# Two stacked attentions on one core: who empties PSUM around the turns between the layers

## Chip, cores and metric

The kernel runs on one core of one Trainium2 chip. The metric is device time in microseconds (us), launch to end; 3021.95 us is the median of three runs before the change (3021.81 to 3022.91). The profiled execution took 3022.45 us, with a span of 3020.7 us, and TensorE had 0.997 of its full clock.

## The reference, cut to what matters

The input `x` is float32, 8 images x 64 channels x 64 x 64, so N = 4096 positions per image.

```python
# layer 0
f, g, hh = Wf @ x + bf, Wg @ x + bg, Wh @ x + bh        # 8, 8 and 64 channels
beta = softmax(f.T @ g, axis=keys)                      # 4096 x 4096 per image
x = x + hh @ beta.T
# layer 1
xn = group_norm(x, 8 groups) * gamma + beta_
q, k, v = split(w_qkv @ xn + b_qkv)                     # 64 channels each
attn = softmax(q.T @ k * 64**-0.5)                      # 4096 x 4096 per image
out = x + w_proj @ (attn @ v) + b_proj
```

## The kernel before, in words

**Tiles.** An image lies in SBUF as 128 partitions x 2048 columns: the 64 channels of the first half of the positions, and below them those of the second half. The 2048 columns are four *chunks* of 512 queries (`CW`), for both halves at once. A chunk takes 16 *steps* `t` (`NT`). One step handles 128 keys of each half: TensorE makes four 128 x 512 blocks of scores, ScalarE turns them into exponentials in an SBUF tile `e` (128 x 2048; the pool holds six, `ppool`), TensorE multiplies them with the values and adds into an accumulator in PSUM (`weigh`), and VectorE adds `e` into a running sum `esum` for the softmax's denominator.

**PSUM.** Of the eight banks, 1 to 6 form three pairs that scores and projections use in turn (`pair`); banks 0 and 7 hold the accumulators (`outer`). Layer 1 needs both, one for each 64 keys; layer 0 needs one and swaps them from chunk to chunk, so that the other serves as a seventh bank for scores.

**Order.** The layers are interleaved: layer 0 of images 0 and 1, then layer 1 of image 0, layer 0 of image 2, layer 1 of image 1, and so on; layer 1 of image 7 ends it. So from 565 us on a *period* repeats: 64 steps of layer 0 of image b, then 64 steps of layer 1 of image b-1. Six times layer 1 is followed by layer 0, and seven times layer 0 by layer 1; these are the *turns*. In the trace the first such period lies from 565.2 to 936.4 us: layer 0 of image 2 until about 706.8 us, layer 1 of image 1 after it. (Layer 1 of image 0 comes ahead of it, from 336.3 us on.)

**Who sets the order.** TensorE's order is written out by hand: each matmul is tied behind the one before (`in_order`). In layer 1 a step issues its scores (L958), its exponentials (L961), and then, in `ended`, the work that is due and the `weigh` of the step before. Layer 0 works in groups of six or seven 512-column blocks of scores, then the due work, then `weigh`. Work beside the main loop is put on a list with a step number (`at_step`) and taken when its step comes (`take`), at most one piece that needs a pair of banks per step; layer 0 looks one step ahead (L976).

**What runs beside layer 1 of an image b-2**, by the step numbers in `before` of both layers: for layer 0 of image b, `begin` at step 25 (it projects f and g with 8 matmuls in `project_all`, L594, copies the result out of PSUM by ScalarE at L608, and splits it on VectorE into a rounded and a rest part, `high`, with two instructions), `spread` at step 28 (twelve transfers that lay f and g out), and `values` at steps 36, 38, 43 and 45; for layer 1 of image b-1, the group norm's statistics from step 20 on, and from step 35 in steps of 7 `project` (L747), followed two steps later by `values`. `values` (L335) is 16 small matmuls into a pair of banks, and one copy of 128 x 512 out of it. The copy goes to VectorE when no pair is lent (`lent is None`), which is always so in layer 1's steps; in layer 0's steps it goes to ScalarE.

**The end of a chunk.** `finish` (L361) calls `total`: in layer 1 two ScalarE copies take the accumulators out of PSUM (L790, L791), and VectorE adds them later, in `halves`. The remaining pieces (`halves`, `transposed`, `reciprocals`, `result`) are due over the next steps; `transposed` and `reciprocals` send small transfers, and `result` waits for `r`, the reciprocals spread by two transfers of 128 KB.

VectorE instructions are recorded by one helper (L141), TensorE's matmuls by another (L151); they are told apart by their tiles. The trace holds two records for each float32 matmul, so that the 8 matmuls of a layer 1 step's scores show as x16.

Of the kernel before, what the change touches and what calls it, by code (L numbers as in the profile page):

```python
# [68 lines left out]
def fast_path(  # L69
# [19 lines left out]
    nc = tc.nc  # L89
# [23 lines left out]
    lent = None  # L113

    def pair():
        nonlocal turn
        if lent is not None:
            return pairs[lent]
        turn += 1
        return pairs[turn % 3]  # L120
# [27 lines left out]
    vector = InOrder()  # L148
# [176 lines left out]
    class Attention:  # L325
# [12 lines left out]
        def values(self, src, w, c):  # L338

            ps = pair()  # L340
            for t in range(TPC):
                for m in range(2):
                    for h in range(2):
                        matmul(
                            ps[ts(m, C), h, ts(t, C)], src[ts(h, C), ds(t * P + m * C, C)],
                            w[ts(h, C), :], start=True, stop=True,
                        )

            first_ = self.kind == self.b == c == 0
            copy = vector.tensor_copy if lent is None or first_ else nc.scalar.copy  # L350
            copy(
                self.vt[:, :, ts(c, TPC), :],
                ps[:, :, 0 : TPC * C].rearrange("k p (t c) -> k p t c", c=C),
            )

        def finish(self, acc, esum, c, index):

            n = f"{self.name}_{c}"
            raw = work.tile([P, CW], F32, tag="raw", bufs=4, name=f"raw_{n}")
            other = self.total(raw, acc)  # L360
            zt = small.tile([P, QP], F32, tag="zt", bufs=4, name=f"zt_{n}")  # L361
            width = CW // 2
            r = four = None

            def halves():
                if other is not None:
                    vector.tensor_add(raw, raw, other)
                vector.tensor_add(esum[:, 0], esum[:, 0], esum[:, 1])

            def transposed():  # L370


                nonlocal four
                both_ = work.tile([P, 8 * QP], F32, tag="zs", name=f"part_{n}")
                part = both_[:, 0:32]
                four = both_[:, 32:].rearrange("p (a k) -> p a k", k=QP)
                vector.tensor_reduce(
                    part, esum[:, 0].rearrange("p h (i b) -> p b (h i)", b=32),
                    axis=AX.X, op=ALU.add, apply_transpose=True,
                )  # L380
                for a in range(4):
                    nc.sync.dma_start(four[:, a, :], part[ts(a, 32), :])

            def sums(spare):

                z = banks[:, spare, :]

                zs = work.tile([P, width], F32, tag="zs", name=f"zs_{n}")
                for h in range(2):
                    for i in range(2):  # L390
                        row = 32 * (2 * h + i)
                        matmul(
                            z[row : row + 32, 0:width], ones[:, 0:32], esum[:, 0, h, ts(i, width)],
                            start=True, stop=True, tile_position=(0, row),
                        )
                nc.scalar.copy(zs, z[:, 0:width])
                for h in range(2):
                    for i in range(2):
                        row = 32 * (2 * h + i)
                        nc.sync.dma_start(zt[row : row + 32, :], zs[row : row + 1, :])  # L400

            def broadcast():
                nonlocal r
                r = work.tile([P, CW], F32, tag="r", name=f"r_{n}")

            def reciprocals():
                rt = stash[:, ts(index, QP)]
                if four is not None:
                    vector.tensor_reduce(
                        zt, four.rearrange("p a k -> p k a"), axis=AX.X, op=ALU.add  # L410
                    )
                vector.reciprocal(rt, zt)
                broadcast()
                dealt = recips[index]
                nc.sync.dma_start(dealt, rt)
                for h in range(2):
                    row = dealt[ts(h, C), :].rearrange("p e -> (p e)")
                    nc.sync.dma_start(r[ts(h, C), :], row.partition_broadcast(C))

            def result():  # L420
                vector.tensor_mul(raw, raw, r)
                self.residual(raw, c)

            return halves, transposed, sums, reciprocals, result
# [52 lines left out]
    class Layer0(Attention):  # L477
# [4 lines left out]
        def before(self):  # L482

            def begin():
                if self.b == 1:
                    self.own(F32R)
                else:
                    self.parts = proj.tile([P, 2, NH], F32R, tag="fg", name=f"fg_{self.name}")  # L490
                    if self.b != 2:
                        self.own_vt()
                self.f, self.g = self.parts[:, 0, :], self.parts[:, 1, :]
                self.st = small.tile(
                    [P, NC, nc.vector.BN_STATS_DIM], F32, tag="st", name=f"st_{self.name}"
                )
                if self.b > 0:
                    self.project_all()
                else:
                    self.project_direct()  # L500
                    self.project(0, (1,))

            def rest():
                self.project(1)
                with tc.issue_after(self.sent.ins):
                    for b in (1, 2):
                        load_x(b)

            if self.b == 0:
                return [(-1, begin, True), (0, rest, True)] + [  # L510
                    (
                        (-1, 1, 5, 8)[c],
                        lambda c=c: self.values(x_tiles[0][:, ts(c, CW)], wh, c),
                        True,
                    )
                    for c in range(NC)
                ]


            s = 28 if self.b == 1 else 25  # L520
            return [(s, begin, True), (s + (4 if self.b == 1 else 3), self.spread, False)] + [
                (
                    (36, 38, 43, 45)[c],
                    lambda c=c: self.values(x_tiles[self.b][:, ts(c, CW)], wh, c),
                    True,
                )
                for c in range(NC)
            ]
# [114 lines left out]
        def weigh(self, acc, e, t, p, start, stop, cols):  # L643
            for h in range(2):
                matmul(
                    acc[0][ts(h, C), cols], self.vt[:, p, t, :], e[:, h, cols],
                    start=start, stop=stop,
                )

        def total(self, raw, acc):  # L650
            nc.scalar.copy(raw, acc[0])
            return None

# [5 lines left out]
    class Layer1(Attention):  # L659
# [124 lines left out]
                        e[ts(m, C), h, cols], start=start, stop=stop,  # L784
                    )

        def total(self, raw, acc):

            other = work.tile([P, CW], F32, tag="r", name=f"other_{self.name}")
            nc.scalar.copy(raw, acc[0])  # L790
            nc.scalar.copy(other, acc[1])  # L791
            return other
# [17 lines left out]
    seq = [(at, c) for at in order for c in range(NC)]  # L810
# [38 lines left out]
    acc = esum = first = None  # L849
# [96 lines left out]
    while i < len(seq):  # L946
        at, c = seq[i]
        tight = i < 2 * NC
        if at.kind == 1:
            for j in range(0, 2 * NT, 2):  # L950
                now = i * NT + j // 2
                due, taken = take(now)
                batch, left = ready, []
                t = j // 2
                new = []
                both_ps = [pair(), pair()]
                for p in range(2):
                    at.scores(both_ps[p], t, p, c)  # L958
                e = ppool.tile([P, 2, 2, CW], F32, tag="e", name=f"e_{at.name}_{c}_{t}")
                for p in range(2):  # L960
                    nc.scalar.activation(e[:, p], both_ps[p], AF.Exp, scale=at.scale)  # L961
                    new.append((i, j + p, e, slice(0, CW)))
                ended()
            i += 1
            continue
# [6 lines left out]
        u = 0  # L972
        while u < len(units):
            k, t = units[u][:2]
            now = k * NT + t
            due, taken = take(now + 1)  # L976
            wide = 7 if closed == 0 and taken != BANK else 6
            batch, left = due_part(ready, wide - (2 if taken == PAIR else 0))
# [8 lines left out]
            if taken == PAIR:  # L987
                lent = 0 if room[-1] == 7 else 2
# [6 lines left out]
            while group:  # L995
                (k, t, p, h), bank = group[0]
                first_ = 2 * p + h
                n_ = min(4 - first_, len(group))
                at, c = seq[k]
# [11 lines left out]
            lent = None  # L1011
        i = last
    now = len(seq) * NT
# [390 lines left out]
```

## Time and profile before

| engine | busy, us | share of the span |
|---|---|---|
| TensorE, matmul | 2984.6 | 99% |
| TensorE, weight load | 1076.8 | 36% |
| VectorE | 2601.0 | 86% |
| ScalarE | 2055.7 | 68% |
| GpSimd | 15.7 | 1% |

| instruction | count | mean, ns |
|---|---|---|
| VectorE `esum` + `e`, 128 x 2048 | 629 | 2288 |
| ScalarE exponential in layer 1, 128 x 1024 | 1024 | 1023 |
| VectorE copy PSUM to `v`, 128 x 512 | 28 | 694 |
| VectorE copy PSUM to `vt`, 128 x 512 | 25 | 695 |
| ScalarE copy PSUM to `v`, 128 x 512 | 8 | 589 |
| ScalarE copies of the accumulators in layer 1 | 31 + 31 | 588, 598 |
| VectorE split of f and g, two instructions | 8 and 7 | 688 and 1285 |

Read it thus: a busy TensorE row is nearly full here whatever happens, because a matmul that has been issued early counts as busy; so a stall shows better in the weight loads (PEld), in the list of waits, and in the distance between one step's exponentials and the next's. VectorE and ScalarE rows are real busy times.

### The profile page before, as it was taken

Reading aid. Unit: us, or ns where it says so; the run is one execution under the profiler, and the core shown is the slowest. Engines: PE = TensorE matmul, PEld = TensorE weight load, DVE = VectorE, ACT = ScalarE, POOL = GpSimd, SP = SyncE. Lnnn points to the kernel's source line nnn. Section 1 sums busy time; section 2 is a strip of 40 time slices with the busy share of each in tenths; the row PEclk is TensorE's granted clock in tenths of the full one; section 3 lists DMA queues with packets and bytes.
Section 4 is the critical chain, followed back from the end, with each engine's and each line's share of the span. In section 5 each row is a group of like instructions: output and inputs, shape, how many; then the busy total and the mean of one; then the engine's idle time right before and its main releaser. Section 6 shows DMA issues by size and latency. Waiting matters only on the chain.

```text
span 3020.7 us, 58290 instructions
## 1 busy us (share of the span) xinstructions
PE 2984.6 (99%) x25629; PEld 1076.8 (36%) x25629; DVE 2601.0 (86%) x1705; ACT 2055.7 (68%) x1979; POOL 15.7 (1%) x40
## 2 busy tenths in 40 slices
PE   8999999999999999999999999999999999999998
PEld 3333333333333333333333333333333333333333
DVE  7999977899878998789987899879997799976776
ACT  6877655786557866578655885568855588566554
POOL 2000000000000000000000000000000000000000
PEclk9999999999999999999999999999999999999999
DMA  2100020100201002010020100200002000010000
GB/s 65 43 8 15 12 51 19 29 1 9 54 19 29 1 13 51 20 29 1 16 51 19 26 1 16 51 23 22 1 16 54 19 8 1 17 23 15 9 15 13
DMA packets 77141, 66.93 MB, mean 22 GB/s; under 512 B 54048, under 2 KB 54080, under 8 KB 75088
## 3 DMA queue, kind: packets, MB, share of 16 engines
q1 hardware_dynamic: 75792, 63.01, 8.7%
q8 instruction: 202, 3.31, 0.5%
q14 instruction: 59, 0.48, 0.1%
q0 software_dynamic: 768, 0.09, 0.0%
q10 hardware_dynamic: 320, 0.04, 0.0%
HBM read 39.84 MB, written 12.32 MB: 17 GB/s over the span
## 4 chain that ended last, share of the span: by engine, by line
PE 89%; DVE 6%; ACT 2%; issue 2%; DMA 0%; SPq 0%; DVEq 0%; ACTq 0%
PE banks L151 89%; DVE esum_l L141 5%; DVE vt_l L141 1%; ACT e_l L961 1%; ACT e_l L1002 1%; DMA x<-in_x_dram 0%; ACT other_l L791 0%; DMA moments<-mv_l 0%; DVE raw_l L141 0%; DVE x L141 0%; DVE st_l L141 0%; ACT full_l L573 0%; DMA zt_l<-zs_l 0%; DVE high_l L141 0%; DMA group_l<-moments 0%
## 5 line engine op out<-in xcount | busy, mean ns | idle before, releaser
L141 DVE TENSOR_TENSOR esum_l<-esum_l,e_l 128x2048 f32<-128x2048 f32 x629 | 1439.4, 2288 | 255.1 <-ACT e_l L961 230.2
L961 ACT ACTIVATE e_l<-banks 128x1024 f32<-128x1024 f32 x1024 | 993.8, 1023 | 733.7 <-PE banks L151 733.7
L151 PE MATMUL banks<-e_l,v_l 64*64 64x512 f32 (+1 forms) x8780 | 1094.0, 587 | 0.0
L1002 ACT ACTIVATE e_l<-banks 128x2048 f32<-128x2048 f32 (+3 forms) x727 | 954.5, 1375 | 180.1 <-PE banks L151 166.4
L151 PE MATMUL banks<-kq_l 64*64 64x512 f32 (+1 forms) x8448 | 1005.3, 586 | 5.7 <-ACT e_l L1002 4.7
L151 PE MATMUL banks<-e_l,vt_l 128*64 128x512 f32 (+1 forms) x4056 | 830.5, 550 | 0.0
L141 DVE TENSOR_TENSOR kq_l<-kq_l,e_l 128x2048 f32<-128x2048 f32 x252 | 577.3, 2291 | 24.8 <-DVE kq_l L141 0.9
L151 PEld LDWEIGHTS banks<-e_l,v_l 64*64 64x64 f32 (+1 forms) x8780 | 347.3, 134 | 593.7 <-issue 517.9
L151 PEld LDWEIGHTS banks<-kq_l 64*64 64x64 f32 (+1 forms) x8448 | 325.3, 134 | 600.3 <-issue 556.7
L151 PEld LDWEIGHTS banks<-e_l,vt_l 128*64 128x64 f32 x4056 | 267.3, 136 | 468.7 <-issue 449.2
L151 PE MATMUL banks<-fg_l 32*128 32x512 f32 x1792 | 206.8, 459 | 6.5 <-ACT e_l L1002 3.3
L141 DVE TENSOR_TENSOR esum_l<-e_l,e_l 128x2048 f32<-128x2048 f32 x45 | 102.3, 2274 | 85.7 <-ACT e_l L961 85.7
L151 PEld LDWEIGHTS banks<-fg_l 32*128 32x128 f32 x1792 | 85.6, 182 | 188.3 <-ACT e_l L1002 138.0
L141 DVE TRANSPOSE_TENSOR_REDUCE part_l<-esum_l 128x32 f32<-128x1024 f32 x38 | 74.5, 1961 | 0.0
L141 DVE TENSOR_TENSOR esum_l<-esum_l 128x1024 f32<-128x1024 f32 x44 | 53.7, 1221 | 0.4
L141 DVE TENSOR_TENSOR raw_l<-raw_l,r_l 128x512 f32<-128x512 f32 x63 | 43.2, 686 | 0.0
L141 DVE TENSOR_TENSOR kq_l<-e_l,e_l 128x2048 f32<-128x2048 f32 x18 | 41.2, 2287 | 1.4 <-ACT e_l L1002 1.4
L141 DVE TRANSPOSE_TENSOR_REDUCE part_l<-kq_l 128x32 f32<-128x1024 f32 x18 | 35.2, 1957 | 0.2
L141 DVE TENSOR_TENSOR vt_l<-vt_l,e_l 128x2048 f32<-128x2048 f32 x14 | 32.1, 2291 | 1.2
L764 ACT ACTIVATE kq_l<-banks,kqb 64x256 f32<-64x256 f32 x64 | 30.0, 469 | 1.2
L151 PEld LDWEIGHTS banks<-wkq_wvp,kq_l 64*64 64x64 f32 x1024 | 19.4, 134 | 28.0 <-DVE vt_l L141 18.0
L151 PE MATMUL banks<-wkq_wvp,kq_l 64*64 64x64 f32 x1024 | 21.4, 221 | 7.5 <-DVE vt_l L141 7.5
(126 smaller groups left out, 475.6 us busy)
## 6 DMA issues: line engine op xcount, KB each, us to landing
r_l<-recips SPq DMA_DIRECT2D x126, 128.0 KB
kq_l<-kq_l SPq DMA_DIRECT2D x64, 128.0 KB
out_dram<-raw_l SPq DMA_DIRECT2D x62, 128.0 KB
x<-in_x_dram SPq DMA_DIRECT2D x30, 256.0 KB
fg_l<-fg_sent_l SPq DMA_DIRECT2D x24, 256.0 KB
fg_l<-fg_sent_l SPq DMA_DIRECT2D x48, 128.0 KB
part_l<-part_l SPq DMA_DIRECT2D x228, 4.0 KB
fg_sent_l<-high_l SPq DMA_DIRECT2D x28, 128.0 KB
```

Source lines behind the costliest of these rows:

```text
L141: it = getattr(nc.vector, name)(*args, **kwargs)
L151: in_order(nc.tensor.matmul(*args, **kwargs))
L764: nc.scalar.activation(self.q[ts(h, C), cols[1]], ps[other, 1, 0:width], AF.Identity, bias=k1["kqb"][other, :],)
L961: nc.scalar.activation(e[:, p], both_ps[p], AF.Exp, scale=at.scale)
L1002: nc.scalar.activation(e.rearrange("k p h n -> k (p h) n")[:, first_ : first_ + n_, :], banks[:, bank : bank + n_, :], AF.Exp, scale=at.scale,
```

## The change

It does four things.

1. `values` leave PSUM by ScalarE in layer 1's steps as well; only the very first copy of the program stays on VectorE. That moves 28 copies to `v` and 24 to `vt`, so that TensorE's next use of the pair does not stand behind VectorE's queue.
2. `begin` for images 2 to 7 moves from step 25 of layer 1 to its step 0, and is taken at the turn; `spread` keeps step 28 in the list.
3. At the turn from layer 0 to layer 1 the last `weigh` of layer 0, and what is due, are issued before the first scores of layer 1, so that f and g are projected where layer 0's last work is.
4. At the turn from layer 1 to layer 0 VectorE takes both accumulators: one copy and one addition that reads the second accumulator from PSUM, in place of two ScalarE copies and a later addition.

```diff
-            first_ = self.kind == self.b == c == 0
-            copy = vector.tensor_copy if lent is None or first_ else nc.scalar.copy
+            copy = vector.tensor_copy if self.kind == self.b == c == 0 else nc.scalar.copy
...
-            other = self.total(raw, acc)
+            other = self.total(raw, acc, index)
...
-            s = 28 if self.b == 1 else 25
-            return [(s, begin, True), (s + (4 if self.b == 1 else 3), self.spread, False)] + [
+            s, spread = (28, 32) if self.b == 1 else (0, 28)
+            return [(s, begin, True), (spread, self.spread, False)] + [
...
-        def total(self, raw, acc):
-
+        def total(self, raw, acc, index):
+            if seq[index + 1][0].kind == 0:
+                vector.tensor_copy(raw, acc[0])
+                vector.tensor_add(raw, acc[1], raw)
+                return None
             other = work.tile([P, CW], F32, tag="r", name=f"other_{self.name}")
             nc.scalar.copy(raw, acc[0])
             nc.scalar.copy(other, acc[1])
...
                 new = []
+                if batch and seq[batch[0][0]][0].kind == 0:
+                    for r in batch:
+                        weigh(*r, now)
+                    for u in due:
+                        u[2]()
+                    due, batch = [], []
                 both_ps = [pair(), pair()]
```

More of the change, by code (lines that the diff above doesn't have):

```diff
@@ L785, in weigh, with total @@
                     )
-        def total(self, raw, acc):
+        def total(self, raw, acc, index):
+            if seq[index + 1][0].kind == 0:
+                vector.tensor_copy(raw, acc[0])
+                vector.tensor_add(raw, acc[1], raw)
+                return None
             other = work.tile([P, CW], F32, tag="r", name=f"other_{self.name}")
```

## The prediction

> **What bounds the kernel now.** I read the page's shares first, then the list of waits, then the timeline of one period.
>
> ```profile
> PE 2984.6 (99%) x25629; PEld 1076.8 (36%) x25629; DVE 2601.0 (86%) x1705; ACT 2055.7 (68%) x1979; POOL 15.7 (1%) x40
> ...
> PE 89%; DVE 6%; ACT 2%; issue 2%; DMA 0%; SPq 0%; DVEq 0%; ACTq 0%
> ```
>
> TensorE sets the pace: 89% of the chain of waits. VectorE's 6% is what a change to VectorE's queue can speak to, not its 86% of busy time. The waits from 430 us on (past the start) say who holds TensorE:
>
> ```profile
> ACT e_l L961 <- PE banks L151: 695.3, 461, 3.2
> ...
> PEld banks L151 <- DVE vt_l L141: 18.0, 12, 1.8
> ...
> PEld banks L151 <- DVE v_l L141: 8.5, 19, 0.7
> DVE raw_l L141 <- ACT other_l L791: 8.0, 6, 1.3
> ...
> PE banks L151 <- DVE vt_l L141: 7.5, 12, 1.0
> ```
>
> Columns: total us, times, longest. ScalarE waits 695 us for TensorE in layer 1, so it has room there. TensorE waits for one thing that is avoidable: VectorE's copies out of PSUM. The twelve `vt` waits are two in each of six layer 1 stages. The timeline shows the larger one (first VectorE, then ScalarE, then weight loads; start, duration, in brackets the idle time before):
>
> ```profile
> 832.51 2.29 DVE L141 TENSOR_TENSOR esum_l<-esum_l,e_l 128x2048 f32<-128x2048 f32 x1
> 834.72 2.00 DVE L141 TRANSPOSE_TENSOR_REDUCE part_l<-esum_l 128x32 f32<-128x1024 f32 x1
> 836.58 2.31 DVE L141 TENSOR_TENSOR esum_l<-esum_l,e_l 128x2048 f32<-128x2048 f32 x1
> 838.75 0.74 DVE L141 COPY vt_l<-banks 128x512 f32<-128x512 f32 x1
> ```
> ```profile
> 837.79 1.94 ACT L961 ACTIVATE e_l<-banks 128x1024 f32<-128x1024 f32 x2 [1.96 <-PE banks L151]
> 842.89 1.94 ACT L961 ACTIVATE e_l<-banks 128x1024 f32<-128x1024 f32 x2 [3.15 <-PE banks L151]
> 846.85 1.02 ACT L961 ACTIVATE e_l<-banks 128x1024 f32<-128x1024 f32 x1 [2.02 <-PE banks L151]
> ```
> ```profile
> 839.54 0.56 PEld L151 LDWEIGHTS banks<-wkq_wvp,kq_l 64*64 64x64 f32 x32 [1.84 <-DVE vt_l L141]
> ```
>
> The copy of 0.74 us sits behind an end-of-chunk reduction and a 2.3 us addition; the next `values` needs the pair. ScalarE meanwhile waits 3.15 us for scores.
>
> **What the Trainium skill says.** "PSUM — Partial Sum Buffer", section Engine vs sequencer instructions: "ScalarE/VectorE/GpSimdE queues are strict FIFO." The lines above agree: the copy starts when the addition ahead of it ends. "Perfetto Trace Analysis", section Optimizing Scalar/DVE Operations, gives ScalarE the smaller access overhead on PSUM (51 against 125 ns). The trace agrees in direction: 589 against 694 ns for the same 128 x 512 copy; I use these. "TensorEngine Tiling (Array Packing)", section Key Properties, says that a change of tiling mode drains TensorE; at the turns below a switch costs some 0.1 to 0.2 us.
>
> **Part 1, values by ScalarE.** In layer 1 the exponentials start 3.43 us apart (e.g. 853.71 to 857.15). A step with `project` or with an undelayed `values` takes 3.86 to 3.90; I take 3.88. The distances around the eight `values` of a period are 3.90, 5.10, 3.96, 3.90, 4.36, 3.90, 3.84 and 3.90, with small after-effects (3.48 for 3.43, twice). Excess: 1.22 + 0.08 + 0.48 + 2 x 0.05, about 1.9 us. Six stages have it (layer 1 of images 0 to 5): **11.4 us**. Bounds: 7.5 us, the matmul row's waits for `vt`; and 17.8, the weight loads' 26.5 us of waits for `vt` and `v` less the 0.28 that each of the 31 has between any two groups. The ScalarE copy itself I cost at nothing: it goes in behind the step's 1.94 us of exponentials, ahead of the next step's scores; ScalarE idles 1.49 us in a plain step, and about 1.9 when `values` lengthens it. 0.59 fits. Behind the copy wait the next exponentials, which wait for scores anyway. The pair comes free about 3.7 us after the step's scores start (1.16 to the first exponential, 1.94, 0.59), while the next `values` cannot come before 3.88 + 1.72 = 5.6.
>
> **Part 4, the turn from layer 1 to layer 0.** The matmuls there:
>
> ```profile
> 568.53 2.80 PE L151 MATMUL banks<-e_l,vt_l 128*64 128x512 f32 x12
> 571.26 1.19 PE L151 MATMUL banks<-fg_l 32*128 32x512 f32 x7
> 572.38 2.80 PE L151 MATMUL banks<-e_l,vt_l 128*64 128x512 f32 x12
> 575.11 0.93 PE L151 MATMUL banks<-fg_l 32*128 32x512 f32 x7
> ```
>
> A group's seven blocks of scores take 0.66 before the next `weigh` when banks are free (586.38 to 587.05). The third group takes 1.12 (571.26 to 572.38): its later blocks wait for exponentials that ScalarE began at 568.83, after its two accumulator copies (567.89 to 568.97). Without these they start near 568.0 and end before 571.26: 0.45 us. The fourth group's 0.86 stays, since ScalarE (seven blocks in 3.22 us plus 0.59 of waiting for scores) is the slower one while groups are short. The second group's 1.39 stays too; it waits for the first exponentials. So **0.43 x 6 = 2.6 us**, between 0 and the whole lost here, 0.7 + 0.45 + 0.2 = 1.4, times six, 8. VectorE gets 0.69 + 0.69 (the same two kinds at the kernel's end take 0.69 each) for an addition of 0.69. In the built instruction order they come behind `halves`, which ends at 567.67; so bank 0 is free near 568.4, as now (568.49), and the 0.69 more fits into the 1.34 us for which VectorE waited there.
>
> **Parts 2 and 3, the turn from layer 0 to layer 1.** At step 25 the projection lengthens a step from 3.43 to 4.61 (exponentials at 794.52 and 799.13): 1.18 us removed. At the turn it costs from 0.86 (a step's eight scores matmuls run four at a time, 0.86 for each four; the projection's eight lie in eight tiles, so once) up to 1.3. No wait hides it: TensorE is full from 703.18 to 714.44. But the order scores, `weigh`, scores, `weigh`, scores, `weigh` becomes scores, projection, the whole `weigh`, two sets of scores; layer 1's first scores lose their 0.16 (1.88 for 1.72) and layer 0's last `weigh` its 0.15 (2.30 for ten half blocks at 0.215). My sum: 10.40 us (0.44 + 0.2 + 0.86 + 0.2 + 5.16 + 0.1 + 3.44, the 0.1s and 0.2s estimates for switches from these rows) for 9.55 + 1.18 = 10.73. **0.33 x 6 = 2.0**, and 0.3 at the seventh turn, which has no projection; bounds -1 and 4. The first scores now have no `weigh` to hide their exponentials, but `weigh` of the first step comes only after two sets of scores, 3.44 us on, and the exponentials end 1.16 + 1.94 = 3.10 us after the first set starts.
>
> VectorE: `high` and its split (1.97 us) move from step 25 to the turn, where VectorE is about 10 us behind (the last layer 0 exponential ends at 705.64, its addition at 716.26). The first layer 1 addition then ends near 723.6 for 721.6. With six `e` buffers, the exponential of layer 1's seventh step needs the first one back, at 729.3: 5 us of room. The spread's transfers are now issued some 80 us earlier, about 725 to 736, near `r` of layer 0's first chunk. Twelve of them drained at about 200 GB/s from 806 to 817 before; I find `r` landing near 740, and VectorE not at its product before 744. Cost nothing.
>
> **Sum**: 11.4 + 2.6 + 2.0 + 0.3 = 16.3, so **3005.7 us**. TensorE's matmuls are the same in number and shape.
>
> **Rivals.**
> - *The wait moves to ScalarE.* If its copies delay exponentials, or the pair is held by the queue ahead of them, part 1 gives little. For: the copy is in order behind 1.94 us of work. Against: 733.7 us of ScalarE's waiting for TensorE. Time: only the 4.9 us of the other parts, less 0 to 4 of new waits: 3017 to 3021.
> - *VectorE blocks at the turn.* If `r` comes 10 us late behind the spread, VectorE stands, the six `e` buffers fill, and ScalarE and TensorE stop for some 5 us each period: 3005.7 + 6 x 5 = 3036. For: VectorE is full from 716 to 771. Against: the 4 us of room worked out above, and 5 us in the buffers.
> - *More than counted*: part 1 at its upper 17.8 and part 4 at 6: 3021.95 - 26 = 2996.
>
> **Chances.** Forecast 0.78, wait moved 0.09, slower 0.06, more than counted 0.07. Range 3000 to 3013: parts 1 and 4 at their likely spread. Faster by over 0.2% (6 us) 0.90, same 0.05, slower 0.05.
>
> **What would show it.** The waits for `vt` and `v` by VectorE gone, and steps of 3.88 for 5.10 and 4.36; the turn's third group at 0.66; no 4.61 step; a turn to layer 1 of about 10.4 us from its last scores. Wrong would be: new waits of TensorE for `v` by ScalarE over 0.3 us, ScalarE waiting for VectorE in layer 1, or VectorE waiting for `r`.

## The result and the profile after

The changed kernel takes **3005.66 us** (median of four runs, 3005.01 to 3006.12); the kernel before took 3021.96 us beside it (3021.81 to 3022.91). The ratio is 0.9945, with an interval of 0.9928 to 0.9962: 16.3 us less.

On the page of the changed kernel the busy times hardly look different; TensorE's row says 99% in both:

```profile
PE 2973.7 (99%) x25629; PEld 1078.7 (36%) x25629; DVE 2574.0 (86%) x1659; ACT 2073.0 (69%) x2019; POOL 16.1 (1%) x40
...
PE 93%; DVE 4%; issue 1%; ACT 1%; DMA 0%; SPq 0%; DVEq 0%; ACTq 0%
```

The chain of waits does look different: TensorE has 93% of it for 89%, VectorE 4% for 6%. TensorE has the same 25629 records, so it does the same work with fewer holes. VectorE has 46 instructions fewer; ScalarE has 40 more (52 copies more, 12 fewer of accumulators).

The waits of the changed kernel from 430 us on (total us, times, longest):

```profile
ACT e_l L972 <- PE banks L151: 645.0, 455, 1.6
...
PEld banks L151 <- ACT e_l L972: 88.8, 313, 0.8
...
PEld banks L151 <- ACT other_l L796: 6.6, 24, 0.3
PEld banks L151 <- ACT kq_l L759: 5.8, 21, 0.3
```

No row of TensorE names `vt` or `v` any more. ScalarE waits 645 us for TensorE where it waited 695, and the longest wait is 1.6 us for 3.2: it is still the engine with room. (The weight loads' waits for `e_l`, 88.8 us for 64.9, are no new stalls of ScalarE's copies: those over 0.35 us, four in all, are loads of `fg_l` at turns to layer 0.)

ScalarE's timeline in layer 1 of image 1, changed kernel, at the same three `values` as the prediction's block from 837.79 on:

```profile
834.80 1.94 ACT L972 ACTIVATE e_l<-banks 128x1024 f32<-128x1024 f32 x2 [1.48 <-PE banks L151]
836.63 0.59 ACT L350 COPY v_l<-banks 128x512 f32<-128x512 f32 x1
838.70 1.94 ACT L972 ACTIVATE e_l<-banks 128x1024 f32<-128x1024 f32 x2 [1.48 <-PE banks L151]
840.53 0.59 ACT L350 COPY vt_l<-banks 128x512 f32<-128x512 f32 x1
842.66 1.94 ACT L972 ACTIVATE e_l<-banks 128x1024 f32<-128x1024 f32 x2 [1.54 <-PE banks L151]
```

Each copy sits in what was idle time: exponentials, copy, then still 1.48 us of waiting for scores. The distances are 3.90 and 3.96, where before one was 5.10.

TensorE at the turn from layer 1 to layer 0 (third group), and at the turn from layer 0 to layer 1, changed kernel:

```profile
569.22 0.73 PE L151 MATMUL banks<-fg_l 32*128 32x512 f32 x7
569.88 2.79 PE L151 MATMUL banks<-e_l,vt_l 128*64 128x512 f32 x12
...
700.66 0.52 PE L151 MATMUL banks<-fg_l 32*128 32x512 f32 x4
701.11 1.09 PE L151 MATMUL banks<-x,wfg 64*32 64x512 f32 x16
702.13 5.38 PE L151 MATMUL banks<-e_l,vt_l 128*64 128x512 f32 x28
707.43 3.66 PE L151 MATMUL banks<-kq_l 64*64 64x512 f32 x32
710.92 1.90 PE L151 MATMUL banks<-e_l,v_l 64*64 64x512 f32 x16
```

The third group's scores take 0.66 us (569.22 to 569.88) for 1.12. The turn to layer 1 takes 10.26 us from layer 0's last scores (700.66 to 710.92), projection included. In the kernel before it took 9.55 without a projection, from the first to the second of these lines:

```profile
703.18 0.52 PE L151 MATMUL banks<-fg_l 32*128 32x512 f32 x4
712.73 1.90 PE L151 MATMUL banks<-e_l,v_l 64*64 64x512 f32 x16
```

**One period is the ruler.** In the chain of waits of the changed kernel each period is one piece of TensorE, after a short one of ScalarE:

```profile
566.06 365.62 PE banks L151 x3137
...
934.55 365.63 PE banks L151 x3128
```

From one to the next it is 368.49 us; the same two places in the kernel before lie 371.25 apart:

```profile
568.06 254.19 PE banks L151 x1848
...
939.31 254.21 PE banks L151 x1846
```

So a period gains 2.76 us, six periods 16.6. The period repeats within 0.02 to 0.04 us from one to the next and between kernels that differ only ahead of it, while the stretch up to 566 us comes out differently by a microsecond or more. The granted clock doesn't blur it: in all but two of the traces below it is 1.00 in every period, and the spells at 0.50 lie in the first 260 us (6.8 to 17.1 us in all, by trace) and at the very end. (The two are those in which VectorE's extra work costs time, below.) Small changes are therefore read below in the period, and the time is given beside it.

### The profile page after: what moved, and what is told of

Its sections match the earlier page's. It is cut to its first block, busy times and chain, and to the rows that moved or that the text cites. A ratio compares the mean times of both kernels' runs of the same rounds, so it can differ in the third digit from the quotient of the medians.

```text
span 3004.0 us, 58286 instructions
## 1 busy us (share of the span) xinstructions
PE 2973.7 (99%) x25629; PEld 1078.7 (36%) x25629; DVE 2574.0 (86%) x1659; ACT 2073.0 (69%) x2019; POOL 16.1 (1%) x40
## 4 chain that ended last, share of the span: by engine, by line
PE 93%; DVE 4%; issue 1%; ACT 1%; DMA 0%; SPq 0%; DVEq 0%; ACTq 0%
PE banks L151 93%; DVE esum_l L141 3%; DVE vt_l L141 1%; ACT e_l L1013 1%; DMA x<-in_x_dram 0%; DVE x L141 0%; DVE raw_l L141 0%; DVE st_l L141 0%; ACT full_l L573 0%; DVE high_l L141 0%; DVE kq_l L141 0%; DVE rt L141 0%; SPq L399 0%; DMA zt_l<-zs_l 0%; DVE w_l L141 0%
## 5 line engine op out<-in xcount | busy, mean ns | idle before, releaser
L651 ACT COPY raw_l<-banks 128x512 f32<-128x512 f32 x32 | 18.9, 590 | 25.2 <-PE banks L151 24.3
L151 PEld LDWEIGHTS banks<-wh,x 64*64 64x64 f32 x1024 | 21.2, 138 | 16.7 <-issue 15.8
```

The lines of the kernel that those rows point to most:

```text
L151: in_order(nc.tensor.matmul(*args, **kwargs))
```

## The experiments

All times are medians; the kernel before took 3021.3 to 3021.5 us beside them.

**The parts, one at a time.** Part 1 alone:

```diff
-            first_ = self.kind == self.b == c == 0
-            copy = vector.tensor_copy if lent is None or first_ else nc.scalar.copy
+            copy = vector.tensor_copy if self.kind == self.b == c == 0 else nc.scalar.copy
```

> Part 1 alone: every values copy but the first by ScalarE, all else as before. If TensorE's wait for its pair behind VectorE's queue is the gain (theory), six layer 1 stages lose about 1.7 us each, as the changed kernel's rest-of-stage shows: 3021.95 - 10.3 = about 3011.7 us (3010.5 to 3013), with the 5.10 and 4.36 us steps at 3.9. If the wait only moves to ScalarE (rival), 3017 to 3021. If the parts only pay together (rival: the turns free VectorE for the copies' sake), over 3014.

Measured: 3011.09 us, ratio 0.9965 (0.9951 to 0.9979). The period is 369.49, so 1.76 less than before.

Part 4 alone:

```diff
+            if seq[index + 1][0].kind == 0:
+                vector.tensor_copy(raw, acc[0])
+                vector.tensor_add(raw, acc[1], raw)
+                return None
```

> Part 4 alone: at six turns from layer 1 to layer 0 VectorE takes the accumulators. Theory: 0.6 us a turn, 0.45 from ScalarE's copies no longer ahead of the exponentials and 0.12 from the first weigh of layer 0 starting a little earlier: 3021.95 - 3.5 = 3018.4 us (3017.5 to 3019.5). Rival, that VectorE's extra 0.69 us shows up as later copies of the values in layer 1 and eats it: 3020 or more.

Measured: 3018.61 us, ratio 0.9991 (0.9984 to 0.9997); period 370.74, 0.51 less. In its trace the third group at the turn takes 0.67:

```profile
570.00 0.74 PE L151 MATMUL banks<-fg_l 32*128 32x512 f32 x7
570.67 2.79 PE L151 MATMUL banks<-e_l,vt_l 128*64 128x512 f32 x12
```

Parts 2 and 3 alone:

```diff
-            s = 28 if self.b == 1 else 25
-            return [(s, begin, True), (s + (4 if self.b == 1 else 3), self.spread, False)] + [
+            s, spread = (28, 32) if self.b == 1 else (0, 28)
+            return [(s, begin, True), (spread, self.spread, False)] + [
...
+                if batch and seq[batch[0][0]][0].kind == 0:
+                    for r in batch:
+                        weigh(*r, now)
+                    for u in due:
+                        u[2]()
+                    due, batch = [], []
```

> Parts 2 and 3 alone: f and g projected at the turn, layer 0's last weigh ahead of layer 1's first scores. Theory, fewer changes of tile shape on TensorE: 0.47 us at each of six turns and about 0.3 at the seventh: 3021.95 - 3.1 = 3018.8 us (3018 to 3020). Rival, that the move pays by taking 1.97 us of split off VectorE ahead of the values: then steps of 5.10 and 4.36 us shrink here too, and the time is under 3016.

Measured: 3018.16 us, ratio 0.9989 (0.9981 to 0.9997); period 370.76, 0.49 less.

Part 3 alone, the last six lines of that diff with `begin` left at step 25:

> Part 3 alone: layer 0's last weigh ahead of layer 1's first scores at seven turns, the projection still at step 25. Theory (changes of tile shape): two of them fewer at each turn, about 0.3 us x 7 = 2.1: 3019.9 us (3019 to 3021), and the rest of the turn's gain belongs to the projection's place. Rival, that without a weigh between them the first two sets of scores wait for PSUM or exponentials: no change or slower, 3022 to 3025.

Measured: 3019.32 us, ratio 0.9993 (0.9984 to 1.0001); the interval touches 1, but the period is clear: 370.90, 0.35 less. Its turn to layer 1 takes 9.24 us from layer 0's last scores (701.77 to 711.01) for 9.55 before:

```profile
701.77 0.51 PE L151 MATMUL banks<-fg_l 32*128 32x512 f32 x4
702.22 5.38 PE L151 MATMUL banks<-e_l,vt_l 128*64 128x512 f32 x28
707.52 3.66 PE L151 MATMUL banks<-kq_l 64*64 64x512 f32 x32
```

So the order `weigh`, scores, scores is worth 0.31 there. With `begin` at the turn it is 10.26: the projection costs 1.02 there, against the 1.18 that its step lost before.

The three parts add up: 1.76 + 0.51 + 0.49 = 2.76 per period, which is what the whole change gains. No interplay between them shows.

**Which copies.** Is the gain of part 1 in the `vt` copies, whose waits led the list? Only those go to ScalarE:

```diff
-            copy = vector.tensor_copy if lent is None or first_ else nc.scalar.copy
+            by_vector = first_ or (lent is None and self.kind == 1)
+            copy = vector.tensor_copy if by_vector else nc.scalar.copy
```

> Of part 1 only the copies for layer 0's values (24 to vt) go to ScalarE; the 28 to v stay on VectorE; all else as before. Theory, that the wait is for a pair whose copy stands behind VectorE's end-of-chunk work and which another values wants one step later: the vt copies carry it (14.6 of the 17.8 us of waits), so 3021.5 - 9 = about 3012.5 us (3011.5 to 3014). Rival, that taking 0.69 us copies off VectorE is what pays: half of part 1, 3016 to 3017.

Measured: 3016.95 us, ratio 0.9985 (0.9979 to 0.9992); period 370.47, 0.78 less. That is a miss of 4.5 us, and it lies where the rival had it, that VectorE's relief is what pays (3016 to 3017). A line of its waits, and of its ScalarE, VectorE and weight load timelines:

```profile
PEld banks L151 <- DVE v_l L141: 16.2, 19, 1.1
```
```profile
837.98 1.94 ACT L962 ACTIVATE e_l<-banks 128x1024 f32<-128x1024 f32 x2 [1.48 <-PE banks L151]
```
```profile
839.95 2.29 DVE L141 TENSOR_TENSOR esum_l<-esum_l,e_l 128x2048 f32<-128x2048 f32 x1 [0.41 <-ACT e_l L962]
842.16 0.68 DVE L141 COPY v_l<-banks 128x512 f32<-128x512 f32 x1
```
```profile
842.89 0.56 PEld L151 LDWEIGHTS banks<-wh,x 64*64 64x64 f32 x32 [1.11 <-DVE v_l L141]
```

The `vt` waits are gone, and those for `v` have grown from 8.5 to 16.2 us. The step distances say the same: the 5.10 and 4.36 fell to 3.90, but the next ones rose from 3.96 and 3.90 to 4.41 and 4.42. VectorE is not late with a backlog here; it waited 0.41 us for the exponentials that its addition reads. It is enough that the copy stands behind this one addition of 2.29 us. On VectorE the copy starts 4.18 us after the step's exponentials (837.98 to 842.16); on ScalarE it stands behind the exponentials alone, and starts after 1.83 (834.80 to 836.63 in the changed kernel). By the prediction's own sum the pair is then free 1.16 + 4.18 + 0.68 = 6.0 us after the step's scores start, and the next `values` can want it after 5.6.

The other half, only `v` to ScalarE (the same edit with `self.kind == 0`):

> Of the change, only layer 1's values (`v`) leave PSUM by ScalarE; layer 0's (`vt`) stay on VectorE. The other half of the run with `vt` alone (-4.4 us). Theory, that in each row of `values` the copies stand in for one another, so that a half gives little by itself: the waits for `vt` stay as they are (5.10 and 4.36 us steps), only the small waits for `v` go; 3018 to 3021. Rival, that the two halves simply add (-10.4 less -4.4 is -6.0): 3015.5.

Measured: 3020.82 us, ratio 0.9999 (0.999 to 1.0007); period 371.19, 0.06 less. The `vt` waits stay as they were:

```profile
PEld banks L151 <- DVE vt_l L141: 18.0, 12, 1.8
```

This also speaks against the relief of VectorE as the cause: 28 of the 52 copies are off its queue, and next to nothing is gained. One half gives 0.78, the other 0.06, both together 1.76. The first `values` of a stage come in rows of three, one in each step (`vt`, `v`, `vt`), and a wait that is taken away uncovers the next copy's.

**Where the copies fall.** Would it have done to move layer 0's `values` off the end of a chunk, and leave all copies on VectorE?

```diff
-                    (36, 38, 43, 45)[c],
+                    (36, 38, 43, 45)[c] if self.b == 1 else (28, 30, 32, 34)[c],
```

> No copy changes its engine: layer 0's values move from steps 36, 38, 43 and 45 of layer 1 to steps 28, 30, 32 and 34, ahead of the end-of-chunk work at 36 and 37 and not next to another values; all else as before. Theory (place in VectorE's queue, with a neighbour that wants the pair at once): nearly all of part 1 comes without ScalarE, 3021.5 - 9 = about 3012.5 us (3011 to 3015). Rival, that ScalarE's faster copy or its idle time is what counts: 3020 or more.

Measured: 3016.57 us, ratio 0.9984 (0.9978 to 0.9991); period 370.43, 0.82 less. Another miss, and for one of its two waits in a stage the reason is the same. Its waits, VectorE and weight loads in the same stage:

```profile
PEld banks L151 <- DVE vt_l L141: 13.0, 12, 1.2
```
```profile
827.97 2.29 DVE L141 TENSOR_TENSOR esum_l<-esum_l,e_l 128x2048 f32<-128x2048 f32 x1 [1.10 <-ACT e_l L961]
830.18 0.68 DVE L141 COPY vt_l<-banks 128x512 f32<-128x512 f32 x1
```
```profile
830.92 0.21 PEld L151 LDWEIGHTS banks<-kq_l,wkq_wvp 64*64 64x64 f32 x8 [1.16 <-DVE vt_l L141]
```

Again VectorE was idle (1.10 us) just before the addition that the copy stood behind, and the next piece wants the pair at once: here it is `project`, at step 35, right after the `values` of step 34. Of the four copies that were moved two make such a wait in each of six stages. The other one that does stands behind a backlog: VectorE is busy without a pause from 801.20 until the copy at 809.39. The two between them (815.52 and 819.94) make none, though the first stands behind an addition as well. There only scores want the pair, 5.6 us after `values` took it (811.90 to 817.51); in a row of `values` it is wanted after 3.9.

So the end-of-chunk reduction made the longest wait of before, 1.8 us, but a copy on VectorE can make TensorE wait 1.0 to 1.2 us without it. These four steps are no full remedy. Whether others would be, further from `project`, no run here shows; ScalarE needs no such choice.

**How much room VectorE has at the turn.** The change puts the split of f and g, 1.97 us, in front of layer 1's first additions there, costed at nothing. More work in that place, the changed kernel with ten more copies of `full` to `high` ahead of the split, images 2 to 7:

```diff
             vector.tensor_copy(high, full)
+            for _ in range(10 if self.b > 1 else 0):
+                vector.tensor_copy(high, full)
```

> The changed kernel, with ten more copies of 0.69 us on VectorE at the split of f and g of images 2 to 7, so 6.9 us more of VectorE's queue at each of six turns to layer 1; the results are the same. The first addition of layer 1 ends at 720.3 in the changed kernel's trace, the exponential that needs its buffer back starts at 727.5: 7.2 us of room, and TensorE stands some 2 us further off. Theory: no change, 3005 to 3008. Rival, that the room is the 5 us or less of the prediction, or that layer 0's reciprocals chain VectorE to the transfers: 3012 or more.

Measured: 3023.15 us, ratio 1.0005 (0.9997 to 1.0014), a miss: 17.5 us above the changed kernel, so all of the gain is lost. The ten copies (0.69 us each in the row of these casts) are 6.9 us. No exponential of layer 1 waits for `esum` there. A wait of its list that was not in the changed kernel, and ScalarE's timeline in layer 1 of image 1:

```profile
ACT other_l L798 <- DVE raw_l L141: 16.9, 5, 3.5
```
```profile
760.93 1.94 ACT L974 ACTIVATE e_l<-banks 128x1024 f32<-128x1024 f32 x2 [1.50 <-PE banks L151]
763.47 0.59 ACT L797 COPY raw_l<-banks 128x512 f32<-128x512 f32 x1 [0.60 <-PE banks L151]
767.23 0.58 ACT L798 COPY other_l<-banks 128x512 f32<-128x512 f32 x1 [3.17 <-DVE raw_l L141]
767.71 1.95 ACT L974 ACTIVATE e_l<-banks 128x1024 f32<-128x1024 f32 x2
```

This is 45 us after the ten copies (they end at 722.65), at the end of layer 1's first chunk. The second accumulator's tile `other` has the pool tag `"r"` and shares its two buffers with layer 0's reciprocals `r`. VectorE, still behind with layer 0's ends of chunks, multiplies `raw` by such an `r` at 766.47, and until that ends (767.15) ScalarE can't write `other`. The exponentials behind it wait too, 6.78 us from one to the next for 3.43. That is the "strict FIFO" of the Trainium skill once more ("PSUM — Partial Sum Buffer", section Engine vs sequencer instructions), on ScalarE this time: the exponential starts at 767.71, when the blocked copy is through (767.81). In the changed kernel that product ends at 761.29 and the copy comes at 764.83: the room is 3.5 us, and 6.9 less 3.5 is the 3.4 us (16.9 over 5) that ScalarE waited. Four of the five periods are 2.95 to 3.34 us longer than the changed kernel's. One is 4.65 longer (17.2 together): there TensorE stands for 2.20 us, until 1139.63, and the clock granted to it is 0.50 from 1139.0 to 1142.5.

Twenty copies, 13.8 us:

> The same with twenty copies, 13.8 us at each of six turns: 6.6 us beyond the 7.2 of room, less about 2 that TensorE has of its own: 4.5 us at five turns and 6 at the first, 3005.7 + 28 = about 3033 us (3022 to 3045). Rival, that VectorE's lag at the turn never reaches TensorE: under 3010.

Measured: 3066.56 us, ratio 1.0147 (1.0132 to 1.0163), 61 us above the changed kernel, and more than the range expected. Its waits have both limits; the third line is the copy to `other` in layer 1 of image 1:

```profile
ACT e_l L974 <- DVE esum_l L141: 78.6, 42, 3.2
...
ACT other_l L798 <- DVE raw_l L141: 36.3, 5, 7.3
```
```profile
774.60 0.59 ACT L798 COPY other_l<-banks 128x512 f32<-128x512 f32 x1 [7.27 <-DVE raw_l L141]
```

The five periods are 11.6 to 13.0 us longer than the changed kernel's, 62 together. TensorE stands for 6.78 us at each of these turns (here until 775.24), and each time the clock granted to it falls to 0.50 while it stands, for 6.8 or 10.2 us (here from 771.1 to 781.3); the two records of a 64x512 matmul take 1.06 us at 777.85, and 0.59 at 783.02. TensorE works for 3.3 to 6.1 us of each such spell, 23 us in all, so that about half of that, 11.5 us, is lost to the clock; this is an estimate from these spells. What is left is 10.1 us a turn, near the 13.8 - 3.5 = 10.3 of the shared buffers. The sixth turn, the first in time, has no wait for `other`. ScalarE waits 8.4 us for `esum` there, but the stage is only 0.6 us longer (223.71 for 223.08 from layer 1's first exponential to layer 0's).

Is it the shared buffer, or VectorE's lateness as such? Ten copies again, with `other` in the buffer of `full`, which is free at that time:

```diff
-            other = work.tile([P, CW], F32, tag="r", name=f"other_{self.name}")
+            other = work.tile([P, 2, CW], F32, tag="full", bufs=1, name=f"other_{self.name}")[:, 0]
```

> The changed kernel with the same ten extra VectorE copies at the turn to layer 1 (6.9 us, images 2 to 7), but layer 1's second accumulator copy (`other`) goes to the buffer of `full`, which is idle there, instead of one of the two that it shares with `r`. Theory, that the shared buffers made the loss of 17.5 us: ScalarE no longer waits for VectorE at L798, and the time falls to 3006 to 3010, the rest being `e` buffers that come back late. Rival, that the ten copies cost by themselves (VectorE's delay reaches TensorE through the `e` buffers anyway): 3018 to 3023, with waits of ScalarE for `esum`.

Measured: 3004.88 us, ratio 0.9945 (0.9931 to 0.9958), period 368.51. The whole loss is gone, a little more than expected, with VectorE's 6.9 us still there; ScalarE copies both accumulators back to back:

```profile
762.65 0.59 ACT L797 COPY raw_l<-banks 128x512 f32<-128x512 f32 x1 [0.60 <-PE banks L151]
763.13 0.59 ACT L798 COPY other_l<-banks 128x512 f32<-128x512 f32 x1
```

So ten copies cost nothing by themselves. The six `e` buffers have room for that much too: in the changed kernel the first addition ends at 720.28, and the exponential that needs its `e` back starts at 727.5, 7.2 us later.

**A faster version?** The chain has VectorE (`esum`, `vt`) for 23% of the first 430 us, where two layer 0 stages follow each other. For the six chunks of layer 0 whose end is not put off, all there, TensorE adds the two halves of `esum` in place of VectorE:

```diff
-                for h in range(2):
-                    for i in range(2):
-                        row = 32 * (2 * h + i)
-                        matmul(
-                            z[row : row + 32, 0:width], ones[:, 0:32], esum[:, 0, h, ts(i, width)],
-                            start=True, stop=True, tile_position=(0, row),
-                        )
+                for k in range(2):
+                    for h in range(2):
+                        for i in range(2):
+                            row = 32 * (2 * h + i)
+                            matmul(
+                                z[row : row + 32, 0:width], ones[:, 0:32],
+                                esum[:, k, h, ts(i, width)],
+                                start=k == 0, stop=k == 1, tile_position=(0, row),
+                            )
...
-        behind(halves)()
```

> The changed kernel; for the chunks of layer 0 whose end is not put off (six of them, all in the first 310 us), the sum of the two halves of `esum` is left to TensorE (eight matmuls instead of four, accumulating) and VectorE's addition of 1.22 us (`halves`) is dropped. If VectorE bounds that stretch, as the chain of waits has it (its longest part there is `esum` on VectorE): 6 x 1.22 = 7.3 less what waits elsewhere, 2998 to 3003. If TensorE bounds it: 6 x 0.43 more, 3008.

Measured: 3002.93 us (3002.55 to 3004.22), ratio 0.994 (0.9926 to 0.9953). The period is 368.50, as it should be; its first period starts at 562.78 for 566.06. About 2.7 us less than the changed kernel, 2.0 if the drift of the kernel before (3021.96 and 3021.27 beside the two) is taken off, and 2.0 also against the run before this one (3004.88), which was timed beside it. Of 7.3 us of VectorE's work less, under half arrives: TensorE's share of the chain up to 430 us rises from 60 to 81%.

Both edits together, without extra copies:

> The changed kernel with both helpful edits of the runs before: no `halves` additions for the first six chunks of layer 0 (2.7 us faster than the changed kernel), and `other` in the buffer of `full` (the run with ten extra copies ended 0.8 us below the changed kernel). No extra copies. Theory: the second edit is worth nothing where no copy is added, since the changed kernel has no wait there: 3002 to 3003.5. Rival: the shared buffers cost something in the changed kernel too: 3001 to 3002.

Measured: 3002.92 us, ratio 0.9937 (0.9923 to 0.9951), period 368.49. The second edit is worth nothing where nothing waits; that the run with ten copies came out 0.8 us below the changed kernel lies in its start (first period from 564.34), not in a period. This version, or the one with the first edit alone, is the fastest measured.

## Why the prediction was right, point by point

The forecast was 3005.7 us, and the time is 3005.66. That the two agree to 0.04 us is luck: the interval of the ratio alone is 10 us wide, and the terms are off by -0.8, +0.5 and +0.9 us and largely cancel:

| term | predicted, each period | measured alone | times six |
|---|---|---|---|
| values by ScalarE | 1.9 | 1.76 | 10.6 for 11.4 |
| turn to layer 0 | 0.43 | 0.51 | 3.1 for 2.6 |
| turn to layer 1 | 0.33 | 0.49 | 2.9 for 2.0 |

- *What bounds the kernel.* Right: each period is one piece of TensorE in the changed kernel's chain, and its gain is the sum of holes closed. VectorE's 86% did not matter.
- *Part 1.* Adding up step distances gave the size; the waits of 26.5 us, from which the upper bound of 17.8 came, did not. What is missing, 0.14, is in my 3.88 us for a step with `values`: the eight are 3.90 to 3.96 in the changed kernel, and sum to some 0.2 more than eight times 3.88. Its explanation was too narrow: I named the reduction at the end of a chunk. The runs with `vt` alone and with other steps show that one addition ahead of the copy is enough where the next piece wants the pair at once, and that the three copies of a row stand in for each other. Had only half of the change been made, that reasoning would have forecast 4.5 us too much.
- *The ScalarE copy costs nothing.* Right: 1.48 us of idle time remain after it, and no wait of TensorE for `v` or `vt` is left in the list.
- *Part 4.* The third group went from 1.12 to 0.66, as worked out. The rest is in the first `weigh` of layer 0, which I had held at no gain: with part 4 alone it starts 3.97 us after the first scores, for 4.02.
- *Parts 2 and 3.* The turn takes 10.26 for the 10.40 of the sum. Without its three switches that sum is 9.90, so by this sum they take 0.36 us together, where I had 0.5: that is 0.14 of the 0.16 by which the term was short. No run measures a switch by itself. (The Trainium skill's "TensorEngine Tiling (Array Packing)", section Key Properties, names the drain, and no size for it.) The seventh turn's 0.3 is there: from layer 0's first exponential of image 7 to layer 1's first of the same image it is 366.86 us before and 366.55 with part 3 alone.
- *5 us of room, cost nothing.* The outcome was right, the step was not. The `e` buffers have 7.2 us, and I had not seen the nearer limit, the buffers that `other` shares with `r`, with 3.5 us. The 1.97 us of the split happen to fit. I looked for who waits for the first addition, not for who waits for everything else that VectorE does later because of it.
- *`r` behind the spread.* I had it land near 740 and the product not before 744. Its transfers are issued at 734.3, among those of the spread (721.6 to 741.1), and VectorE makes the product at 739.83 with no wait for it. So the 4 us between the two, on which I leaned, were not there. It cost nothing all the same: VectorE waits for `r` 0.2 us in the whole stretch from 430 us on.
- *Rivals.* The wait did not move to ScalarE. VectorE blocking at the turn is real, but it needs 3.5 us more work than the change brings, and comes through a buffer, not through `r`. More than counted would have needed the list's 17.8 us.

## What to carry to other kernels

Price a wait by the distances between the steps around it, not by the list's total: a list names who came last, and when that one is taken away the next in the row takes its place (0.78 and 0.06 for the halves, 1.76 for both). A copy that frees PSUM belongs on the engine that comes to it first: both have the step's exponentials to wait for, and VectorE an addition of 2.29 us behind them. How soon the bank is wanted again decides whether that matters. Moving four of the copies to quieter steps of the busy engine gave under half. When work is put on an engine with room, follow every buffer it gives back later, tiles that share a pool tag too: here 6.9 us cost nothing when `other` had another buffer, and 17.5 us where it shared those of `r`.

## What the runs showed that I had not expected

- A period of 368.5 us repeats to within 0.04 us between periods, and between kernels and runs that differ only ahead of it, so that gains of 0.35 us each are clear in one trace where the times' interval touches 1.
- The three parts add up (1.76 + 0.51 + 0.49 = 2.76, closer than the 0.04 us by which a period varies), while the two halves of one part do not add up at all.
- A stall can cost more than it lasts. In each of the five stalls of 6.78 us the clock granted to TensorE fell to half, for 6.8 or 10.2 us, and cost about 2.3 us more each time (the estimate above); in the stalls of 1.86 to 2.24 us, with ten copies, that came once in five.
